# Sparse adjacency products by half blocks of 64 rows: two column parts of TensorE instead of one, in a two-layer graph network

## The chip, the cores and the metric

The kernel runs on one core of a Trainium2 chip. The core has five engines that work at once, each with its own in-order queue: TensorE (matmuls, in the profile PE, with its weight loads PEld), VectorE (DVE), ScalarE (ACT), GpSimd (POOL) and SyncE (SP), which only issues DMAs. The metric is the device time of one execution in microseconds, as the median over runs.

## What is computed

There are N = 2708 nodes with D = 256 features. Layer 0 is a dense graph product with an almost empty adjacency matrix (about 0.3 % of its entries and the diagonal are set):

```
support = adj @ x
x = layernorm(x + relu(concat([x, support]) @ weight + bias))
```

Layer 1 takes the result through two steps. In each, `Xf` goes through R, the adjacency with its identity, rows normalized, and `Xa` goes through an attention matrix A that keeps, in each row, only the largest probabilities whose mass reaches 0.9:

```
for n in range(2):
    A  = top_p_attention(Xa, W1, W2, W3)      # softmax, cut at mass 0.9, rows normalized
    Xf = R @ Xf
    Xa = A @ Xa
    Z  = Z + Xf @ U1[n].T + Xa @ U2[n].T
x = layernorm(x + layernorm(x + Z))
```

Here R = adj + I with each row divided by its sum. The kernel pulls the U1 products forward: with yf = x1 U1[1]ᵀ and v = x1 U1[0]ᵀ, the whole share of R is R (v + R yf). So there are two rounds over R with 256 columns each: s = 0 makes R yf and adds it to v, s = 1 makes R v.

## The kernel before

**Blocks.** Rows are cut into NB = 22 blocks of P = 128; the last one, EDGE, has 20 rows. All data is fp32. One fp32 matmul leaves two records in the trace.

**Stage 0 (layer 0).** For each block m the dense products of adj run on PE (`adj_product`), while DVE looks which 128 x 128 column groups are occupied (`name_columns`): for each block m of 128 rows, and for each of the 128 x 21 other nodes, whether any of the block's rows uses it. DVE then picks the occupied names out in rounds of eight (`Lists.take`, CAP = 160 names a part, two lists: blocks 0 to 15 and 16 to 21). POOL joins the parts to one list a block (`Lists.end`) and loads it back as `ix`: up to 7 columns (CC) of 128 (CW) node names. So R's block of 128 rows needs at most 896 columns instead of 2708.

**Step 1.** For each of the 22 attention blocks: logits on PE, the cut on DVE, transposes of the kept probabilities on PE (`turn`), their copy on ACT (line 530), products with x1 on PE (`products`, line 564). Beside them POOL gathers R's columns for each block by 7 indirect DMAs of 128 rows of 512 bytes from adj (`adj_gather`, line 367), and SP stores them packed (`adj_store`) in `adjc_d`. Each block ends in a chain `ends`: scale, transpose, projections to the queries and keys of step 2. `ya_pair` makes `ya` = Xa U2[1]ᵀ, two blocks at a time; 11 of them stand around the last block's chain.

**Step 2.** The loop `for per in range(NB + 2)` is a software pipeline. In period `per` the block `per - 2` is transposed and multiplied on PE, `per - 1` and `per` are searched and masked on DVE, and `per + 1` and `per + 2` are searched on ACT and exponentiated. A period has NG = 6 slots. The order of the work on each engine is written out by hand and is the program order.

**R in step 2.** A block of R is 8 matmuls of 128 x 128 by 128 x 256 (7 gathered column groups and the block's own diagonal one), 8 units in the text's count. `r_units(n)` places them in single units over the slots, as `units` says: two blocks ahead of the loop, one each in periods 0 and 1, 18 units a period in periods 2 to 9, none in period 10, 16 a period in periods 11 to 21. In slot 0 they stand ahead of the transposes. The rows of y that belong to the gathered columns are fetched by POOL: 7 indirect DMAs of 128 rows of 1024 bytes (`y_load`, line 719) into one of two slots of `yg`, for block m + 1 when block m begins. The adjacency part comes back by SP (`a_load`). When a block's last unit is placed, `r_out` is queued two slots on: it scales and adds the result, and in round 0 stores v. Round 1's first gather has to wait for all of v.

**Finals.** In round 1, `arrive` adds the parts; `final_slot` takes two rows' blocks a period through two layer norms. `middle` gives POOL two tensor operations a block (lines 1207 and 1208), in POOL's queue with the gathers; `stats` of both norms stand in slot 3 on DVE.

```
            n = n_r * (g + 1) // NG - n_r * g // NG
            ...
            if g == 0:
                if b_exp:
                    shift(b_exp, lg[0])
                r_units(n)
            ...
                turn(t_mul, g, ya, accs[t_mul], e2(t_mul))
```

**What sets the order.** DVE's two long operations of a period are `mask` (line 1088) and `below_level` (line 1023); `mask` releases the next block's transposes on PE, these the copies on ACT.

Of the kernel before, what the change touches and what calls it, by code (L numbers as in the profile page):

```python
# [38 lines left out]
CAP = 160  # L39
ML = 16  # L40
CW, CC = 128, 7
# [11 lines left out]
def gnn_two_layer_kernel(ctx: ExitStack, tc: tile.TileContext, N, xT_d, x_d, adj_d, w0_d, b0_d,  # L53
# [31 lines left out]
    assert NB == 3 * KS + 1 and CW == P and CAP % 8 == 0 and N < NB * P  # L85
# [16 lines left out]
    c.part_d = dram.tile([NB, KS, CAP + 1], FP, name="part_d")  # L102
    c.list_ds = [dram.tile([b - a, KS * CAP], I32, name="list_d") for a, b in ((0, ML), (ML, NB))]
    c.adjc_d = dram.tile([NB, CW, CC * P], FP, name="adjc_d")
# [15 lines left out]
    NF = 6 * NB + 4  # L120
# [28 lines left out]
def fast_path(ctx, tc, c, flags, fint, xT_d, x_d, w0_d, b0_d, w1_d, w2_d, w3_d, u1_d, u2_d, g_d, b_d):  # L149
# [43 lines left out]
    xT = big.tile([P, DC, N], FP, tag="Y", name="xT")  # L193
# [42 lines left out]
    def edge_sum(acc, n, stop=True, meanwhile=None):  # L236

        p = rows(EDGE)
        four = work.tile([P, 4, P], FP, tag="wT", name="four").rearrange("p k i -> p (k i)")
        nc.scalar.copy(four[:, :n], acc[:, :n])  # L240
        if meanwhile:
            meanwhile()
        whole = ps_misc() if meanwhile else ps_acc()
        nc.tensor.matmul(whole[:p, :n], lhsT=fold[:, :p], rhs=four[:, :n], start=True, stop=stop)
        return whole
# [21 lines left out]
    names = room[:, :NB * (NB - 1)].rearrange("p (m c) -> p m c", c=NB - 1)  # L267
    at = NB * (NB - 1)
    ramp = room[:, at:at + NB]
    some = room[:, at + NB:at + 2 * NB]  # L270
    LROOM = 3 * P + 2 * CAP + 1 + KS * (CAP + 1)
    first_room = room[:, at + 2 * NB:at + 2 * NB + LROOM]
# [6 lines left out]
    ix = small.tile([P, NB, CC], I32, tag="ix", name="ix", bufs=1)  # L279
    nc.gpsimd.iota(ix.rearrange("p m c -> p (m c)"), pattern=[[0, NB * CC]], base=LAST, channel_multiplier=0)  # L280
    for i, (a, b) in enumerate(((0, ML), (ML, NB))):
        nc.gpsimd.dma_start(out=c.list_ds[i][:, :CW * CC].rearrange("m (p c) -> p m c", c=CC), in_=ix[:, a:b, :])
    before_m = small.tile([NB, 1], FP, tag="before_m", name="before_m", bufs=1)
# [3 lines left out]
    def name_columns(m):  # L287
        for h in range(2):
            nc.vector.tensor_reduce(some[:, h * KH:(h + 1) * KH], adj_of[m][h], AX.X, ALU.max,
                                    apply_absolute_value=True)  # L290
        nc.vector.tensor_scalar(some, some, 0.0, None, op0=ALU.not_equal)
        for a, b, o in ((0, m, 0), (m + 1, NB, -1)):
            if a < b:
                nc.vector.scalar_tensor_tensor(names[:, m, a + o:b + o], ramp[:, a:b], -float(m * P * NB),
                                               some[:, a:b], op0=ALU.add, op1=ALU.mult)

    class Lists:


        def __init__(self, a, b, flag, room):  # L300
            self.a, self.b, self.n, self.flag = a, b, KS * (b - a), flag
# [22 lines left out]
        def end(self):  # L324
# [9 lines left out]
            nc.gpsimd.dma_start(out=c.part_d[a:b].rearrange("m s k -> (m s) k"), in_=self.out[:n])  # L334
            nc.gpsimd.dma_start(out=self.all, in_=c.part_d[a:b])
            run = small.tile([NB, KS], FP, tag="run", name="run", bufs=1)[:b - a]
            to = small.tile([NB, KS], I32, tag="to", name="to", bufs=2)[:b - a]
# [4 lines left out]
            list_d = c.list_ds[a > 0]  # L342
# [5 lines left out]
            nc.gpsimd.dma_start(out=ix[:CW, a:b, :], in_=list_d[:, :CW * CC].rearrange("m (p c) -> p m c", c=CC))  # L348

    adj_rows = adj_d.rearrange("m p k i -> (m p k) i")  # L350
    staged = {}

    to_turn = []

    def name_y():
        while to_turn:
            m = to_turn.pop()
            nc.gpsimd.tensor_scalar(ix[:CW, m, :], ix[:CW, m, :], m * P * NB, P * NB - 1, op0=ALU.subtract, op1=ALU.min)

    def adj_gather(m):  # L360
# [4 lines left out]
        name_y()  # L365
        for i in range(CC):
            nc.gpsimd.indirect_dma_start(out=a[:CW, i, :], out_offset=None, in_=adj_rows,  # L367
                                         in_offset=bass.IndirectOffsetOnAxis(ap=ix[:CW, m, i:i + 1], axis=0))
        nc.gpsimd.tensor_tensor(a[:p, CC, :], a[:p, CC, :], ident[:p], op=ALU.add)
        to_turn.append(m)  # L370
        staged[m] = a

    def adj_store(m, h):

        i = (CC + 1) // 2
        if h == 0:
            nc.sync.dma_start(out=c.adjc_d[m, :, :i * P], in_=staged[m][:CW, :i, :].rearrange("p c i -> p (c i)"))
            return
        a = staged.pop(m)
        nc.sync.dma_start(out=c.adjc_d[m, :, i * P:], in_=a[:CW, i:CC, :].rearrange("p c i -> p (c i)"))  # L380
        nc.sync.dma_start(out=c.own_d[m, :rows(m), :], in_=a[:rows(m), CC, :])
# [64 lines left out]
    lists = Lists(0, ML, flags[:, NF - 4:NF - 2], first_room)  # L446
    for m in range(NB):
# [18 lines left out]
        if m == ML:  # L466
# [16 lines left out]
        if m >= ML:  # L483
            i = m - ML
            lists.take(CAP // 8 * i // (NB - ML), CAP // 8 * (i + 1) // (NB - ML))
    assert not weights
    lists.end()
    y_room = big.tile([P, DC * N], FP, tag="Y", name="yg")
    YW = 2 * (CC + 1) * D
    yg = y_room[:, :YW].rearrange("p (s c d) -> p s c d", s=2, d=D)  # L490
    spares = [y_room[:, YW + D * i:YW + D * (i + 1)] for i in range(4)]
    lists = Lists(ML, NB, flags[:, NF - 2:], yg[:, 1].rearrange("p c d -> p (c d)"))
# [216 lines left out]
    r_now = []  # L709
    r_in, a_in, y_in = {}, {}, {}  # L710
    arrived, loads, held = {}, {}, {}
    later = [[], []]
    ready = []

    def y_load(s, m):
        y = yg[:, m % 2]
        rows_d = (c.yf_d, c.v_d)[s].rearrange("p k d -> (p k) d")
        for i in range(CC):
            nc.gpsimd.indirect_dma_start(out=y[:CW, i, :], out_offset=None, in_=rows_d,  # L719
                                         in_offset=bass.IndirectOffsetOnAxis(ap=ix[:CW, m, i:i + 1], axis=0))  # L720
        y_in[s, m] = y

    def a_load(m):
        a = adjp.tile([P, KH, P], FP, tag="adj", name="adj_t")
        nc.sync.dma_start(out=a[:CW, :CC, :].rearrange("p c i -> p (c i)"), in_=c.adjc_d[m])
# [3 lines left out]
    def r_load(s, m):  # L729
# [5 lines left out]
        nc.sync.dma_start(out=y[:rows(m), CC, :], in_=(c.yf_d, c.v_d)[s][:rows(m), m, :])  # L735
        r_in[s, m] = a_in.pop(m), y

    def r_units(n):
        for _ in range(n):
            s, m = r_queue[0]  # L740
            p = rows(m)
            if not r_now:
                r_now[:] = [ps_misc(), 0]
                if m + 1 < NB:
                    r_load(s, m + 1)
            acc, k = r_now
            a, y = r_in[s, m]
            kw = CW if k < CC else p
            nc.tensor.matmul(acc[:p, :D], lhsT=a[:kw, k, :p], rhs=y[:kw, k, :], start=k == 0, stop=k == CC)  # L749
            r_now[1] += 1  # L750
            if k == CC:
                r_now.clear()
                r_queue.pop(0)
                r_in.pop((s, m))
                base = za_load(m) if s else v_load(m)
                later[1].append(lambda s=s, m=m, acc=acc, base=base: r_out(s, m, acc, base))
# [6 lines left out]
    def za_load(m):  # L763
# [6 lines left out]
        base = work.tile([P, D], FP, tag="in", name="base", bufs=3)  # L770
# [3 lines left out]
    def r_out(s, m, acc, base):  # L774
        p = rows(m)
        if s == 0:
# [3 lines left out]
            if m == NB - 1:  # L780
                r_load(1, 0)
        else:
            arrive(m, base, acc, rinv[:p, m:m + 1])

    def arrive(m, base, part, scale):

        p = rows(m)
        if base is None:
            h = base = held.pop(m)
        else:  # L790
# [940 lines left out]
```

## Time and profile before

| | us |
|---|---|
| median of 3 runs (lowest, highest) | 1311.74 (1306.66, 1311.86) |
| profiled execution | 1361.88 |
| its span | 1360.1 |
| mean granted TensorE clock | 0.969 |

Busy time by stage, from the windows view of the profiled execution (us):

| stretch | what | PE | DVE | ACT | POOL |
|---|---|---|---|---|---|
| 0 to 288 | layer 0 | 273.7 | 157.5 | 32.0 | 5.5 |
| 288 to 345 | first logits, U1 | 53.1 | 37.3 | 28.3 | 17.5 |
| 345 to 748 | step 1 | 381.7 | 295.0 | 222.9 | 218.2 |
| 748 to 1050 | step 2, to period 10 | 265.1 | 230.0 | 223.3 | 189.9 |
| 1050 to 1321 | step 2, periods 11 to 21 | 254.3 | 253.5 | 219.9 | 202.8 |
| 1321 to 1360 | the end | 22.2 | 24.9 | 7.5 | 1.5 |

A busy PE is not a PE at its peak: the end of a matmul is modelled and the records overlap. POOL's busy time leaves out a gap of 0.30 us before each gather.

### The profile page before, as it was taken

How to read it: one execution, taken by the hardware profiler on the slowest of the kernel's cores; microseconds unless marked ns; L12 is line 12 of the kernel's file. 1: busy time of each engine (PE TensorE's matmuls, PEld its weight loads, DVE VectorE, ACT ScalarE, POOL GpSimd, SP SyncE). 2: the span in 40 equal slices, each digit the busy share in tenths (PEclk: the TensorE clock that was granted, in tenths of full speed). 3: DMA queues.
4: the chain of work that ended last, by engine and by line, in shares of the span. 5: the costliest groups of instructions: out<-in, count | busy, mean ns of one | idle time of the engine just before them, and what ended most of it. 6: DMA issues, size and time to landing. Idle time of an engine off the chain costs nothing.

```text
span 1360.1 us, 18883 instructions
## 1 busy us (share of the span) xinstructions
PE 1250.1 (92%) x5764; PEld 895.5 (66%) x5764; DVE 998.1 (73%) x3406; ACT 733.8 (54%) x1337; POOL 635.2 (47%) x594
## 2 busy tenths in 40 slices
PE   8999999988999999999997959999996999999985
PEld 6877877733567777666774727766664776666763
DVE  2544545866888888877840469878877899999995
ACT  1011011035455565555553577877786898998931
POOL 1000000014554533777563177777743668888850
PEclk9999999989899999999998969999998999999997
DMA  6554545513222110232222245645543444554541
GB/s 186 163 176 155 166 155 160 165 54 117 81 92 67 55 57 10 89 94 95 69 73 74 68 150 157 188 140 175 172 111 109 148 159 143 171 181 151 169 111 33
DMA packets 101993, 166.27 MB, mean 122 GB/s; under 512 B 17394, under 2 KB 74358, under 8 KB 101882
## 3 DMA queue, kind: packets, MB, share of 16 engines
q1 hardware_dynamic: 75596, 108.91, 24.7%
q0 software_dynamic: 20544, 51.17, 13.6%
q10 hardware_dynamic: 5742, 4.89, 1.3%
q8 instruction: 48, 0.79, 0.2%
q14 instruction: 63, 0.52, 0.1%
HBM read 130.87 MB, written 34.03 MB: 121 GB/s over the span
## 4 chain that ended last, share of the span: by engine, by line
PE 67%; ACT 19%; DVE 6%; issue 4%; another core or an unknown queue 2%; DMA 0%; ACTq 0%; DVEq 0%
PE acc L564 22%; PE acc L257 15%; PE lg L507 8%; PE tr L527 5%; PE misc L749 5%; ACT e L969 4%; ACT e L966 3%; ACT e L844 3%; ACT wT L530 3%; PE acc L651 2%; PE acc L462 2%; PE misc L426 2%; PE misc L392 2%; PE acc L672 2%
## 5 line engine op out<-in xcount | busy, mean ns | idle before, releaser
L530 ACT COPY wT<-tr 128x512 f32<-128x512 f32 (+2 forms) x258 | 131.7, 518 | 254.7 <-PE tr L527 153.3
L564 PE MATMUL acc<-ya,wT 128*128 128x256 f32 (+1 forms) x924 | 234.6, 394 | 18.8 <-ACT wT L530 12.1
L564 PE MATMUL acc<-x,wT 128*128 128x256 f32 (+1 forms) x924 | 234.6, 393 | 13.2 <-ACT wT L530 12.9
L719 POOL DMA_INDIRECT yg<-v_d,ix x154 | 190.1, 1234 | 79.4 <-issue 32.3
L564 PEld LDWEIGHTS acc<-x,wT 128*128 128x128 f32 (+1 forms) x924 | 167.2, 192 | 87.8 <-issue 40.6
L719 POOL DMA_INDIRECT yg<-yf_d,ix x154 | 192.6, 1250 | 62.3 <-issue 36.2
L564 PEld LDWEIGHTS acc<-ya,wT 128*128 128x128 f32 (+1 forms) x924 | 169.8, 193 | 75.6 <-issue 28.1
L257 PE MATMUL acc<-y,adj_t 128*128 128x257 f32 (+1 forms) x924 | 208.4, 381 | 0.0
L367 POOL DMA_INDIRECT adj_t<-in_adj,ix x154 | 170.3, 1106 | 51.4 <-issue 42.4
L749 PE MATMUL misc<-yg,adj_t 128*128 128x256 f32 (+1 forms) x704 | 183.5, 395 | 11.4 <-issue 6.6
L257 PEld LDWEIGHTS acc<-y,adj_t 128*128 128x128 f32 (+1 forms) x924 | 171.8, 189 | 32.7 <-issue 8.9
L507 PE MATMUL lg<-k,q 64*128 64x512 f32 (+3 forms) x528 | 151.9, 602 | 29.7 <-issue 11.2
L749 PEld LDWEIGHTS misc<-yg,adj_t 128*128 128x128 f32 (+1 forms) x704 | 125.7, 191 | 61.7 <-issue 31.2
L527 PE MATMUL tr<-ident,e 128*128 128x128 f32 (+2 forms) x946 | 147.0, 274 | 2.3 <-DVE e L1088 2.3
L527 PEld LDWEIGHTS tr<-ident,e 128*128 128x128 f32 (+2 forms) x946 | 113.6, 139 | 41.5 <-issue 17.6
L334 POOL DMA_DIRECT2D part_d<-e x1 | 0.6, 576 | 286.2 <-DVE e L333 286.2
L966 ACT ACTIVATE e<-e,st 128x2708 f32<-128x2708 f32 (+1 forms) x43 | 113.6, 2641 | 0.1
L570 DVE MAX8 cand<-e 128x8 f32<-128x170 f32 (+1 forms) x352 | 87.6, 318 | 32.7 <-ACT e L514 15.4
L969 ACT ACTIVATE e<-e,st 128x2708 f32<-128x2708 f32 (+1 forms) x42 | 110.9, 2641 | 0.1
L439 ACT COPY x1T<-tr 128x256 f32<-128x256 f32 (+1 forms) x22 | 8.0, 364 | 186.6 <-PE tr L438 186.6
L1030 DVE MAX8 cand<-w 128x8 f32<-128x136 f32 (+1 forms) x440 | 106.2, 285 | 0.0
L507 PEld LDWEIGHTS lg<-k,q 64*128 64x128 f32 (+1 forms) x528 | 39.3, 183 | 64.2 <-issue 35.6
(237 smaller groups left out, 1762.9 us busy)
## 6 DMA issues: line engine op xcount, KB each, us to landing
adj_t<-in_adj SPq DMA_DIRECT2D x44, 704.0 KB
adj_t<-adjc_d SPq DMA_DIRECT2D x44, 448.0 KB
adjc_d<-adj_t SPq DMA_DIRECT2D x22, 256.0 KB
base<-za_d SPq DMA_DIRECT2D x41, 128.0 KB
adjc_d<-adj_t SPq DMA_DIRECT2D x22, 192.0 KB
xt<-in_x ACTq DMA_DIRECT2D x21, 128.0 KB
x_d<-x SPq DMA_DIRECT2D x21, 128.0 KB
x1b_d<-xb SPq DMA_DIRECT2D x21, 128.0 KB
```

The costliest lines, as they stand in the source:

```text
L257: nc.tensor.matmul(acc[:p, :n], lhsT=halves[k // KH][:kw, k % KH, :p], rhs=y[:kw, k, :n], start=k == 0, stop=stop and k == NB - 1)
L367: nc.gpsimd.indirect_dma_start(out=a[:CW, i, :], out_offset=None, in_=adj_rows, in_offset=bass.IndirectOffsetOnAxis(ap=ix[:CW, m, i:i + 1] ...
L507: nc.tensor.matmul(lg[:p, h, :b - a], lhsT=q[o, t * P:t * P + p], rhs=keys[s][o, i, :b - a], start=True, stop=True)
L527: nc.tensor.transpose(tr[:kw, k % 4, :p], e[:p, k * P:k * P + kw], ident[:p, :p])
L530: nc.scalar.copy(wT[:, :full, :p], tr[:, :full, :p])
L564: nc.tensor.matmul(acc[:p, :D], lhsT=wT[:kw, k % 4, :p], rhs=y[:kw, k, :], start=k == 0, stop=k == NB - 1)
L570: nc.vector.max(dst[:p, i * 8:(i + 1) * 8], src[:p, i * step:i * step + w])
L719: nc.gpsimd.indirect_dma_start(out=y[:CW, i, :], out_offset=None, in_=rows_d, in_offset=bass.IndirectOffsetOnAxis(ap=ix[:CW, m, i:i + 1], ...
L749: nc.tensor.matmul(acc[:p, :D], lhsT=a[:kw, k, :p], rhs=y[:kw, k, :], start=k == 0, stop=k == CC)
L966: nc.scalar.activation(scr[:b.p, :N], e, AF.Relu, bias=b.nz, scale=b.l[k], accum_out=b.relu)
L969: nc.scalar.activation(scr[:b.p, :N], e, AF.Sign, bias=b.nz, scale=b.l[k], accum_out=b.sign)
L1030: nc.vector.max(b.cand[:p, 8 * i:8 * i + 8], low[:p, SEG2 * i:SEG2 * (i + 1)])
```

## The change

R's block of 128 rows is taken as two parts of 64. Each part has a column list of its own, of at most 4 x 128 names. On PE the two parts' matmuls stand in turn, one for PSUM rows 0 to 63 and one for rows 64 to 127, so on two column parts of the array; the own diagonal group stays one 128 x 128 matmul. A block has then 4 + 4 gathered column groups of 64 instead of 7 of 128. What goes with it:

- Three lists instead of two, of 9, 9 and 4 blocks with twice the rows; CAP falls from 160 to 96, so 12 rounds a list instead of 20. `Lists.end` is split into `end`, `gather`, `join` and `columns`, which stand apart in the program.
- `adj_gather` makes 8 gathers of 256-byte rows instead of 7 of 512-byte rows (4 for EDGE); the packed adjacency is 256 KB a block instead of 448 KB.
- `y_gather` makes 8 gathers of 128 x 1024 bytes a block (4 for EDGE) instead of 7, all in step 2 but those of round 0's first two blocks, as before.
- `r_block` places a whole block in one slot, after that slot's transposes, instead of units in every slot; `r_slots` says which slots. Block m loads m + 2 when it has been placed, into the slot of `yg` that it has read. Round 0 now ends in period 10, slot 4; round 1 has one block in period 11, three in 12, and two a period (slots 1 and 4) after that.
- The last block's chain of step 1 runs ahead of the `ya_pair`s; 5 of these follow after the first logits of the loop, 6 stand in period 0, one a slot. The buffers `e4` and `scr` in their tile come only with period 1 (`fifth`).
- The `stats` of the second norm move from slot 3 to slot 4.

```diff
-CAP = 160
-ML = 16
-CW, CC = 128, 7
+CAP = 96
+LISTS = ((0, 9), (9, 18), (18, 22))
+HP = 64
+CW, CC = 128, 4
+NQ = 2 * CC
...
+        def columns(self):
+            a, b = self.a, self.b
+            for g in range(2):
+                nc.gpsimd.tensor_scalar(ixa[:CW, a + g:b:2, :], ix[:CW, a + g:b:2, :], 2, g, op0=ALU.mult, op1=ALU.add)
+            for m in range(a // 2, b // 2):
+                own = ix[:CW, 2 * m:2 * m + 2, :]
+                nc.gpsimd.tensor_scalar(own, own, m * P * NB, P * NB - 1, op0=ALU.subtract, op1=ALU.min)
...
+    def parts(m):
+        return [(k, g, 2 * k + g) for k in range(CC) for g in range(2 if rows(m) > HP else 1)]
...
-        for i in range(CC):
-            nc.gpsimd.indirect_dma_start(out=a[:CW, i, :], out_offset=None, in_=adj_rows,
-                                         in_offset=bass.IndirectOffsetOnAxis(ap=ix[:CW, m, i:i + 1], axis=0))
+        flat = a.rearrange("p k i -> p (k i)")
+        for k, g, i in parts(m):
+            nc.gpsimd.indirect_dma_start(out=flat[:CW, HP * i:HP * (i + 1)], out_offset=None, in_=adj_rows,
+                                         in_offset=bass.IndirectOffsetOnAxis(ap=ixa[:CW, 2 * m + g, k:k + 1], axis=0))
...
+    def y_gather(s, m, y):
+        rows_d = (c.yf_d, c.v_d)[s].rearrange("p k d -> (p k) d")
+        for k, g, i in parts(m):
+            nc.gpsimd.indirect_dma_start(out=y[:CW, i, :], out_offset=None, in_=rows_d,
+                                         in_offset=bass.IndirectOffsetOnAxis(ap=ix[:CW, 2 * m + g, k:k + 1], axis=0))
...
-    def r_units(n):
-        for _ in range(n):
-            s, m = r_queue[0]
-            p = rows(m)
-            if not r_now:
-                r_now[:] = [ps_misc(), 0]
-                if m + 1 < NB:
-                    r_load(s, m + 1)
...
-            nc.tensor.matmul(acc[:p, :D], lhsT=a[:kw, k, :p], rhs=y[:kw, k, :], start=k == 0, stop=k == CC)
...
+    def r_block():
+        s, m = r_queue.pop(0)
+        p = rows(m)
+        acc = ps_misc()
+        a, y = r_in.pop((s, m))
+        flat = a.rearrange("p k i -> p (k i)")
+        for k, g, i in parts(m):
+            w = min(p, HP)
+            nc.tensor.matmul(acc[HP * g:HP * g + w, :D], lhsT=flat[:CW, HP * i:HP * i + w], rhs=y[:CW, i, :],
+                             start=k == 0, stop=False)
+        nc.tensor.matmul(acc[:p, :D], lhsT=a[:p, CC, :p], rhs=y[:p, NQ, :], start=False, stop=True)
+        if m + 2 < NB:
+            r_load(s, m + 2)
+        base = za_load(m) if s else v_load(m)
+        later[1].append(lambda: r_out(s, m, acc, base))
...
+    second.join(nc.gpsimd)
+    second.columns()
...
-            acc = edge_sum(acc, D, meanwhile=ya_pair)
+            acc = edge_sum(acc, D)
...
-        ya_pair()
         f()
-    ya_pair()
     for t in range(3):
         exps2(blocks[t], 2, *logits(1, t, 2))
-        ya_pair()
-    while y_pairs:
-        ya_pair()
...
         if i == 3:
-            for k, f in enumerate(new + finals):
+            for k, f in enumerate(new):
                 f.stats(k)
+        if i == 4:
+            for k, f in enumerate(finals):
+                f.stats(len(new) + k)
...
-    each = NB * (CC + 1)
-    first = 2 * (CC + 1)
-    units = {0: CC + 1, 1: CC + 1}
-    rest = each - first - sum(units.values())
-    units.update({p: rest * (p - 1) // 8 - rest * (p - 2) // 8 for p in range(2, 10)})
-    units.update({p: each * (p - 10) // 11 - each * (p - 11) // 11 for p in range(11, 22)})
+    first = 2
+    r_slots = {0: (), 1: (2, 5)}
+    r_slots.update({p: (1, 4) for p in range(2, 11)})
+    r_slots[11] = (5,)
+    r_slots.update({p: (1, 4) if p > 12 else (1, 3, 5) for p in range(12, 22)})
...
-    r_units(first)
+    while len(y_pairs) > NG:
+        ya_pair()
...
     for per in range(NB + 2):
+        if per == 1:
+            fifth()
...
-                r_units(n)
...
+            if g in r_slots.get(per, ()):
+                r_block()
...
+            if per == 0:
+                ya_pair()
...
+            if per == 0 and g >= NG - first:
+                r_block()
```

## The prediction

> **What bounds the kernel now.** I read the windows by stage first, then the costliest groups on the page, then the timelines of POOL, DVE and PE in one late period of step 2, since all that the change does to the products lies in step 2 (748 to 1360). In the groups, the products that are to become cheaper stand beside the gathers that feed them:
>
> ```profile
> L719 POOL DMA_INDIRECT yg<-v_d,ix x154 | 190.1, 1234 | 79.4 <-issue 32.3
> ...
> L719 POOL DMA_INDIRECT yg<-yf_d,ix x154 | 192.6, 1250 | 62.3 <-issue 36.2
> ...
> L749 PE MATMUL misc<-yg,adj_t 128*128 128x256 f32 (+1 forms) x704 | 183.5, 395 | 11.4 <-issue 6.6
> ```
>
> The reader should see two costs of like size: 183.5 us of PE for R, and 382.7 us of POOL for its y, with 141.7 us of idle before the gathers. Is that idle free time? The timeline of POOL with DVE's two long operations (start, length, engine, line) says mostly no:
>
> ```profile
> 1144.79 0.95 POOL L719 DMA_INDIRECT yg<-v_d,ix  x1 [0.30 <-issue]
> ...
> 1145.56 3.04 DVE L1088 SCALAR_TENSOR_TENSOR e<-w,st,e 128x2720 f32<-128x2720 f32 x1
> ...
> 1146.04 3.38 POOL L719 DMA_INDIRECT yg<-v_d,ix  x1 [0.30 <-PE acc L564]
> ...
> 1149.72 0.95 POOL L719 DMA_INDIRECT yg<-v_d,ix  x1 [0.31 <-issue]
> ...
> 1151.56 3.04 DVE L1023 SCALAR_TENSOR_TENSOR w<-e,st 128x2720 f32<-128x2720 f32 x1
> ...
> 1152.22 3.21 POOL L719 DMA_INDIRECT yg<-v_d,ix  x1 [0.30 <-issue]
> ```
>
> A gather costs 0.95 and a constant 0.30 before it, so 1.25 us; the one that meets a long DVE operation ends 0.8 us after that operation does and loses 2.43 or 2.26 us. In this period (1145 to 1170) POOL has 14 gathers (17.5), 4.7 of such loss and four tensor operations of the finals (about 3.0 over a normal gap): 25.2 us, and the period, from mask to mask, is 25.2 us. POOL is full. It is not what PE waits for yet, as blocks' last gathers end some 5 us before their first product. PE and ACT have another loop, seen in the same period: mask ends at 1148.6, then
>
> ```profile
> 1148.64 1.99 PE L564 MATMUL acc<-ya,wT 128*128 128x256 f32 x8
> ...
> 1150.47 1.03 PE L749 MATMUL misc<-yg,adj_t 128*128 128x256 f32 x4
> ...
> 1151.34 0.60 PE L527 MATMUL tr<-ident,e 128*128 128x128 f32 x4
> ...
> 1151.97 0.58 ACT L530 COPY wT<-tr 128x512 f32<-128x512 f32 x1 [2.64 <-PE misc L749]
> ```
>
> R's two units in slot 0 stand between mask and the transposes that ACT waits for. So the late periods have two limits at 25.2: this loop, and POOL.
>
> **What the Trainium skill says.** "SBUF — State Buffer", section "SBUF: two separate sides": GpSimd writes the descriptors of its own DMAs, and a VectorE operation that holds the shared port locks it out until it ends. The trace agrees (3.38 against 0.95 us). "Perfetto Trace Analysis", section "Per-instruction lifecycle", wants GpSimd timed from start to start; so I use 1.25 and not 0.95. "TensorEngine Tiling (Array Packing)", section "Key Properties": different tiles of the array run in parallel, and a change of tiling mode drains it. The trace has column parts of 32, for EDGE in layer 0, against the full width:
>
> ```profile
> 29.08 10.02 PE L257 MATMUL acc<-y,adj_t 128*128 128x257 f32 x44
> ...
> 276.62 4.66 PE L254 MATMUL acc<-y,adj_t 128*20 128x257 f32 x44 [3.53 <-issue]
> ```
>
> Both have 44 records; the second, half of it at half clock, takes less than half. Parts do run side by side. No run here shows parts of 64.
>
> **The change, part by part.**
>
> *Products on PE.* Back to back a record starts every 0.216 us, so a matmul is 0.43 and a block 8 x 0.43 = 3.46 us. After: four pairs at 0.43 and the own group 0.43, 2.16 us, and two changes of mode. After the 64-row logits the first record comes 0.09 late and the next 0.10 late, so 0.2 each: 2.56 us. Saved: 0.9 a block, 40 us of PE over 44 blocks. From both sides: with free changes 57 us; if the halves do not overlap, 9 x 0.43 + 0.4 = 4.3 us, a loss of 37. I take 40. None of it is time by itself: PE has gaps in step 2. What reaches the path is slot 0, now without R: 4 records, 0.87 us in a late period, 6 records, 1.3 us, in an early one. Against it a whole block delays `products` in slots 1 and 4 by 2.6 us, which ACT's long activations (2.64 us each) cover there; without that cover it costs 1.2 us a slot over the 3 units there now.
>
> *Gathers of y.* 8 instead of 7 a block, 4 for EDGE: 344 instead of 308, 36 x 1.25 = 45 us more on POOL. Periods: early, 16 x 1.25 + 5.2 = 25.2 us, against 18 units now, 15.75 x 1.25 + 5.2 = 24.9. Early periods last 26.2 on average (836.9 to 1046.9), so nearly nothing is won or lost. Late, 16 x 1.25 + 4.7 + 3.0 = 27.7 against 25.2: +2.5 a period. Two slots of yg let POOL run at most two blocks ahead, so PE waits in `r_block` soon after period 12, which takes three blocks. Behind PE's wait stand the transposes, behind these ACT's copies and DVE's next mask.
>
> *The sum of POOL from block 2's first gather (776.0) to the last (1309.4).* Now 294 gathers, 368 us; losses to DVE 382.7 - 308 x 0.946 = 91; finals 28 (13.9 + 13.8): 487 of 533, so 46 idle, 21 of them between the rounds. After: 328 gathers, 410; the same 91 and 28; and between the rounds what can't be avoided, the landing (1.5, estimated from the packets of the gathers before), the block 2.6, two slots to `r_out` 8, the store and load 2: 14. Sum 543. The first of these gathers waits for block 0, now in period 0, slot 4, which I put at 780. So the last gather ends at 1323; landing and block bring 1327. From R's last product to the end now 1360.1 - 1316.7 = 43.4; it moves from slot 5 to slot 4, +4. End 1374, +14 on the span, 1376 on the profiled execution's 1361.9.
>
> *The last block's chain ahead of the ya pairs.* It is late now by the pairs between its steps: the logits of line 507 at 759.7 could come at 752. DVE's first search at 763 moves to 755. The 19 us of pairs are partly hidden by ACT and DVE in period 0, at 6 x 0.58 = 3.5 us of ACT. Worth 5 to 8 us at period 1, but R's gathers then set the pace from 780, so I count 0 with POOL bound and 7 without.
>
> *Lists, adjacency, SP, stats.* Rounds of names: 36 instead of 40 at 1.1 us, 12 instead of 20 of them in step 1, where PE (17 us a block) is the longer: 0; without that cover, 9 us won. The wait of DVE at 292 for `part_d` (5.0) goes, before a DVE wait of 11.8 for ACT that takes it up: 0. Adjacency gathers 172 instead of 154, +22 us of POOL in step 1, where it is busy 218 of 403: 0. The `join` of the second list puts 7 scatters (some 2.2 us apart) ahead of the first gathers; stores stand 4 slots later, SP waits there and nobody for it. Bytes of `a_load` fall. Stats in slot 4 give the finals on POOL 4 us more: 0.
>
> *To the median.* The profiled execution is 50 us above it. If the two shrink alike the forecast is 1311.7 + 14 = 1326. If the 50 us come out of waits in step 2 in proportion (612 of 1360 us, so 22), POOL's idle falls to 24 and the change costs 36: 1348. I take in between, 1332.
>
> **Rivals.** *POOL has room (28 %), faster.* If gathers cost 1.1 us or less outside the profiled execution, 16 fit into 25.2 (17.6 + 7.7 = 25.3). That is the point from which it decides. Then: 7 at the start, 9 x 1.3 in early and 11 x 0.87 in late periods, 28 us: 1284. For it: the missing 50 us, and R's products never wait for a gather in late periods. Against: the spacing is constant to 0.01 us and the engine never pauses. *POOL absorbs it (12 %), same.* The 46 us idle take the 45 us; the last gather ends where it does now: 1312. Against: the gap between the rounds and the two-block limit. *Halves one after the other (5 %), slower:* PE +37 on top of POOL, 1350. For it only that the trace shows parts of 32, not 64.
>
> **Numbers.** POOL binds: 55 %, 1332, own range 1319 to 1352. Faster by over 0.5 %: 0.28; within 0.5 %, about what a measurement of this kernel can tell from no change: 0.12; slower 0.60. The range from 1284 to 1352 leaves out about 1 in 10 on each side.
>
> **What would show it.** POOL without idle from period 1 to the last gather, late periods near 27.7, PE waiting before R's first product of a block and ACT and DVE behind it; L749's group (r_block's line) near 110 us; two records of a pair starting together. Wrong, if late periods stay under 25.2 or gathers follow each other faster than 1.25.

## The result, and the profile after

The changed kernel takes 1371.85 us (median of 4 runs, 1369.1 to 1374.35), the kernel before 1311.8 (4 runs, 1306.66 to 1312.17): a ratio of 1.0471, 95% interval 1.0446 to 1.0497. It is 60 us slower; 1332 was forecast, with 1352 as the end of the range. Its profiled execution took 1369.5 us (span 1367.7), so this record lies 2 us under its median, where that of the kernel before lay 50 us above. Record against record the change costs 8 us; run against run 60. That difference is the first thing to explain.

The groups of the page after, for R's products and their gathers:

```profile
L752 POOL DMA_INDIRECT yg<-yf_d,ix x172 | 205.0, 1192 | 105.7 <-PE misc L784 63.5
L752 POOL DMA_INDIRECT yg<-v_d,ix x172 | 207.5, 1206 | 68.4 <-issue 33.6
...
L784 PE MATMUL misc<-yg,adj_t 128*64 128x256 f32 (+1 forms) x688 | 120.8, 425 | 34.0 <-DMA yg<-v_d,ix 25.3
```

POOL has 412.5 us of gathers instead of 382.7; the products of the parts take 120.8, and the own groups (line 786, 88 records) 34.2 more, against 183.5. PE now waits more for rows. Three of its waits (engine, line, what ended the wait: us in total, times, longest):

```profile
...
PE misc L784 <- DMA yg<-v_d,ix: 25.3, 22, 3.1
PE misc L415 <- DMA xT<-in_xT: 15.8, 1, 15.8
PE misc L784 <- DMA yg<-yf_d,ix: 8.3, 13, 2.3
```

The second of these three has nothing to do with R. Here is the timeline of a late period after (start, length, engine, line), to set beside the one shown of before:

```profile
1163.57 3.04 DVE L1129 SCALAR_TENSOR_TENSOR e<-w,st,e 128x2720 f32<-128x2720 f32 x1
...
1164.82 2.61 POOL L752 DMA_INDIRECT yg<-v_d,ix  x1 [0.30 <-DMA yg<-v_d,ix]
...
1169.96 3.04 DVE L1064 SCALAR_TENSOR_TENSOR w<-e,st 128x2720 f32<-128x2720 f32 x1
1170.23 3.60 POOL L752 DMA_INDIRECT yg<-v_d,ix  x1 [0.30 <-issue]
1171.84 1.52 PE L784 MATMUL misc<-yg,adj_t 128*64 128x256 f32 x12
...
1175.38 0.95 POOL L752 DMA_INDIRECT yg<-v_d,ix  x1 [0.31 <-issue]
1175.63 0.91 PE L784 MATMUL misc<-yg,adj_t 128*64 128x256 f32 x2 [2.27 <-DMA yg<-v_d,ix]
...
1190.85 3.04 DVE L1129 SCALAR_TENSOR_TENSOR e<-w,st,e 128x2720 f32<-128x2720 f32 x1
```

From the start of one mask to that of the next, an interval in what follows, it is 27.3 us. POOL goes from gather to gather, 1.25 us apart (1174.13, 1175.38, 1176.63 and on); the two that meet DVE's long operations take longer. PE places six products (twelve records) and stops 2.3 us for the next column. This interval and the two before it last 27.3 us each although the mean granted clock of TensorE was 0.87, 0.94 and 1.00 in them. So they do not hang on PE's pace; POOL, which has no pause, is the bound, as forecast.

### The profile page after: what moved, and what is told of

Read it like the earlier page. It is cut to its first block, busy times and chain, and to the rows that moved or that the text cites. A ratio compares the mean times of both kernels' runs of the same rounds, so it can differ in the third digit from the quotient of the medians.

```text
span 1367.7 us, 19110 instructions
## 1 busy us (share of the span) xinstructions
PE 1230.9 (90%) x5839; PEld 842.8 (62%) x5839; DVE 993.9 (73%) x3403; ACT 737.3 (54%) x1337; POOL 683.5 (50%) x663
## 3 DMA queue, kind: packets, MB, share of 16 engines
q1 hardware_dynamic: 76546, 95.32, 21.6%
## 4 chain that ended last, share of the span: by engine, by line
PE 74%; DMA 9%; ACT 6%; DVE 4%; issue 4%; POOL 3%; ACTq 0%; POOLq 0%; DVEq 0%
PE acc L599 26%; PE acc L259 15%; PE lg L542 9%; PE tr L562 6%; PE misc L784 5%; DMA yg<-v_d,ix 4%; DMA yg<-yf_d,ix 3%; PE acc L686 2%; POOL yg L752 2%; PE misc L786 2%; PE acc L486 2%; PE misc L449 2%; PE misc L415 2%; DMA xT<-in_xT 1%; PE misc L734 1%
## 5 line engine op out<-in xcount | busy, mean ns | idle before, releaser
L752 POOL DMA_INDIRECT yg<-yf_d,ix x172 | 205.0, 1192 | 105.7 <-PE misc L784 63.5
L752 POOL DMA_INDIRECT yg<-v_d,ix x172 | 207.5, 1206 | 68.4 <-issue 33.6
L599 PE MATMUL acc<-x,wT 128*128 128x256 f32 (+1 forms) x924 | 230.5, 388 | 0.0
L392 POOL DMA_INDIRECT adj_t<-in_adj,ixa x172 | 176.6, 1027 | 59.6 <-issue 46.9
L542 PE MATMUL lg<-k,q 64*128 64x512 f32 (+3 forms) x528 | 158.3, 625 | 42.5 <-ACT e L884 34.8
L784 PE MATMUL misc<-yg,adj_t 128*64 128x256 f32 (+1 forms) x688 | 120.8, 425 | 34.0 <-DMA yg<-v_d,ix 25.3
L784 PEld LDWEIGHTS misc<-yg,adj_t 128*64 128x64 f32 (+1 forms) x688 | 54.5, 148 | 103.0 <-DMA yg<-v_d,ix 41.0
```

Of the source, the lines that this page charges most:

```text
L392: nc.gpsimd.indirect_dma_start(out=flat[:CW, HP * i:HP * (i + 1)], out_offset=None, in_=adj_rows, in_offset=bass.IndirectOffsetOnAxis(ap=i ...
L542: nc.tensor.matmul(lg[:p, h, :b - a], lhsT=q[o, t * P:t * P + p], rhs=keys[s][o, i, :b - a], start=True, stop=True)
L599: nc.tensor.matmul(acc[:p, :D], lhsT=wT[:kw, k % 4, :p], rhs=y[:kw, k, :], start=k == 0, stop=k == NB - 1)
L784: nc.tensor.matmul(acc[HP * g:HP * g + w, :D], lhsT=flat[:CW, HP * i:HP * i + w], rhs=y[:CW, i, :], start=k == 0, stop=False)
```

## The experiments

The kernels of one group of runs ran on one chip; each group also timed the kernel before. In the first group it took 1366.9 us, in the three later ones 1311.75, 1311.9 and 1310.5. Times are compared within a group, or between groups in which the kernel before took the same to 1.5 us.

**The kernels themselves, again.** No edit.

> The kernel before, once more and unchanged, with its own records. Its timed executions took 1306.7 to 1312.2 us, but the one that was profiled first took 1361.9 us, 50 us more. Theory A (that execution was an odd one, and its step 2 held about 50 us that the timed ones do not have): this record has a span near 1310 us, and its late periods of step 2 are then shorter than 25.2 us. Theory B (recording makes the kernel before slower and leaves the changed one alone): the span is near 1360 us again while the timed median stays near 1311 us.

> The changed kernel once more and unchanged, timed beside the kernel before on one chip. On the chip of the first four runs the kernel before took 1366.9 us (1311.8 where the change was first timed), and ScalarE stood still for 8 to 22 us at the same places of its program (its 277th, 459th and 829th instruction) in both variants of the changed kernel, each time until a train of 16 to 32 gathers on POOL had ended. Theory F (such trains hold back what ScalarE needs to go on, and a chip differs in how much): if the kernel before is near 1367 here, the changed kernel is near 1525 (the 1510 of the kernel with the three-dimensional xT, and 16 for the start); if before is near 1312, it is near 1372 and has no such stall. Rival (the chip costs both kernels the same 55 us): 1427.

> The kernel before once more, for its records on the chip of these runs. Theory F: ScalarE's longest stall outside layer 0 is about 8 us, at its 743rd instruction, at the end of a train of 14 gathers, if the time is near 1367, and there is no stall over 5 us if the time is near 1312.

In the first group the kernel before took 1367.4 (ratio 0.9996, 0.9967 to 1.0025), in the second 1310.8; the changed kernel took 1373.6 there (ratio 1.0462, 1.0432 to 1.0493). Neither theory A nor B of the first run holds. The recorded execution of the first group, 1376.2, lies among the others (1361.4 to 1377.3), so recording adds nothing that can be seen; the chips differ. The record that the forecast was made from most likely comes from a chip like the first group's: its span is like theirs, and its intervals follow that group's record to 0.1 us in many places (26.12, 27.55, 26.05 against 26.11, 27.55, 26.15). What differs can be read from ScalarE's waits. The record before:

```profile
ACT wT L530 <- PE tr L527: 153.3, 94, 5.4
ACT wT L530 <- issue: 35.0, 17, 4.1
...
ACT wT L530 <- remote: 20.6, 6, 8.2
```

The same program on the second group's chip:

```profile
ACT wT L530 <- PE tr L527: 223.3, 132, 5.9
```

"issue" and "remote" are waits that end with nothing that the record holds, 55.6 us together. In the second record ScalarE has no such wait after 300 us. The sum is no account of the 50 us, since the waits for PE's transposes are 70 us longer in the second record. Where the 51 us between the spans lie can be read from the stages: 14 in step 1 (first to last masking, line 635: 384.9 and 370.5), 17 from there to the first mask of step 2, 18 in the ten intervals that follow the first (24.17 us each for seven of them; 26.2 on average in the first record), and none in the late ones.

So only the records of the second group (spans 1309.1 and 1371.5) show the change:

| stretch | before | after | difference |
|---|---|---|---|
| to step 1's first masking | 323.5 | 340.4 | +16.9 |
| step 1, to the last masking | 370.5 | 370.9 | +0.4 |
| to the first mask of step 2 | 81.1 | 85.6 | +4.5 |
| first interval between masks | 30.6 | 33.9 | +3.3 |
| the next ten | 241.2 | 243.7 | +2.5 |
| the twelfth | 24.2 | 37.9 | +13.7 |
| the other nine | 213.0 | 234.0 | +21.0 |
| from the last mask to the end | 25.0 | 25.1 | +0.1 |

By POOL: its first gather of step 2 that waits for a block of R starts at 753.5 before and 784.2 after; from there to the end of the last gather are 506.6 and 536.7; after that, 49.0 and 50.6. The expectation that tied the stalls of ScalarE to the chip held as far as it was put to the test: with the kernel before near 1312 the changed one takes 1373.6, and ScalarE has no wait after 300 us that ends with nothing. On a chip of 1367 the changed kernel itself was not run.

**The loads of xT.** The first row of the table is a part of the diff that was not in the forecast at all:

```diff
-    xT = big.tile([P, DC, N], FP, tag="Y", name="xT")
+    xT = big.tile([P, YT], FP, tag="Y", name="xT")[:, :DC * N].rearrange("p (c n) -> p c n", n=N)
```

SyncE's seven issues of these loads on the timeline, and its waits; before (second group), then the changed kernel:

```profile
0.75 3.70 SPq L196 DMA_DIRECT2D xT<-in_xT  x7
```

```profile
0.75 20.96 SPq L200 DMA_DIRECT2D xT<-in_xT  x7
...
SPq L200 <- DMA xT<-in_xT: 18.2, 6, 3.3
```

Six of the seven wait for the one before to land. Two kernels test the cause: the changed one with three dimensions again, and the kernel before with a flat tile.

```diff
-    xT = big.tile([P, YT], FP, tag="Y", name="xT")[:, :DC * N].rearrange("p (c n) -> p c n", n=N)
+    xT = big.tile([P, DC, YT // DC], FP, tag="Y", name="xT")[:, :, :N]
```

> The changed kernel, with the tile that xT is loaded into declared in three dimensions again (128 x 2 x 2816, of which the first 2708 columns of each half are used) instead of a flat row cut and refolded; the room stays as large. Theory S (the flat tile makes each of the seven loads of xT wait for the one before it: they were issued 3.3 to 3.6 us apart there, 0.4 us apart before): the loads are issued within 5 us again, the first products go on without the 15.9 us gap, and the time falls by 14 to 17 us, to about 1356. Rival (the loads merely move, and the adjacency loads behind them on SP's queue set the start anyway): 0 to 4 us, so 1368 to 1372.

> The changed kernel with the three-dimensional tile for xT, as in the second run, now to be read beside a kernel before of about 1312 us. The sum of the two records made on one chip (spans 1309.1 and 1371.5) is: POOL's first gather of step 2 after block 0's products starts at 753.5 before and 784.2 after (+30.7: 16 from the seven loads of xT, 15 from R's first two blocks standing behind the last block's chain), the stretch from there to its last gather's end is 506.6 and 536.7 (+30.1: 34 more gathers, less the idle they fill), and 49.0 and 50.6 follow. Theory S: the 16 us come back whole, 1357 (1354 to 1360). Rival (the stretch that POOL fills starts no earlier, since something else sets it): 1366 to 1374.

> The kernel before with nothing changed but the tile of xT, declared as one flat row per partition and refolded, as the change does. Theory S (each load of xT then waits for the one before it): 14 to 17 us slower than before, all of it ahead of 40 us. Rival (hidden by layer 0's other loads): 0 to 4 us.

In the third group the three-dimensional tile gives 1358.5 (ratio 1.0359, 1.0324 to 1.0395), 15 us less than the changed kernel's 1373.6 of the second group (the kernel before took the same in both), and the loads go out together:

```profile
0.75 3.75 SPq L200 DMA_DIRECT2D xT<-in_xT  x7
```

That is theory S. The flat tile alone does nothing, though: 1310.25 (0.9996, 0.9981 to 1.0011), issues in 3.71 us; this expectation failed. Of the three forms that ran, only the flat row that is cut out of a longer one and refolded makes the loads wait. That form was not put into the kernel before, and why it makes them wait is not shown.

In the first group the same kernel took 1510.0 us (1.1046, 1.0996 to 1.1096), 151 more than in the third. Its timeline at the longest stall:

```profile
403.61 0.19 ACT L648 ACTIVATION_READ_ACCUMULATOR e<-e,nmax 128x1 f32 x1
...
421.61 0.95 POOL L392 DMA_INDIRECT adj_t<-in_adj,ixa  x1 [0.30 <-issue]
425.39 0.58 ACT L565 COPY wT<-tr 128x512 f32<-128x512 f32 x1 [21.59 <-remote]
```

ScalarE stands 21.6 us with its input ready, while POOL ends a train of 24 gathers, and goes on 2.8 us after the last. What it lacked is not in the record.

**The number of gathers.** In the kernel before, an eighth gather a block into a column that nobody reads (`y_load`); in the changed one, the eighth left out and its column zero, so that those names are missing from R's products.

```diff
+        nc.gpsimd.indirect_dma_start(out=eighth[:CW], out_offset=None, in_=rows_d,
+                                     in_offset=bass.IndirectOffsetOnAxis(ap=ix[:CW, m, 0:1], axis=0))
```

```diff
         for k, g, i in parts(m):
+            if i >= 7:
+                continue
```

> The kernel before, with an eighth gather of y for every block (its first list again, into a column that nobody reads): 44 gathers more on POOL, no other engine has more work. Theory P (POOL's gathers set the pace of step 2, now and before): 40 of them lie in the stretch that POOL fills, so 40 x 1.25 = 50 us at most, 30 to 50 us, 1342 to 1362. Theory E (TensorE and ScalarE's loop sets the pace before, POOL has room): within 6 us of before, 1306 to 1318.

> The changed kernel without the eighth of its eight gathers of y for every block; the column of y that it filled holds zeros instead, so the names of that part are left out of R's products (which are all still issued). 43 or 44 gathers fewer on POOL. Theory P: 30 to 50 us less than the changed kernel, 1322 to 1342. Theory Q (what costs is that a block's products come in one slot and wait there, and POOL is not the bound): within 10 us of the changed kernel, 1362 to 1374.

The eighth gather costs the kernel before 45 us (1411.85 against 1366.85; 1.0342, 1.0311 to 1.0372), and its late intervals go from 25.2 to 27.7, by just two gathers of 1.25. That is theory P; TensorE and ScalarE's loop does not hide more gathers. Both kernels ran on the slower chip; on the other this was not measured. The other run (1470 to 1494) says nothing: it was in the first group too, without the changed kernel beside it, and shows the same stalls of ScalarE (22.9 us at 423).

**One slot.** The kernel before with a block's eight products placed together:

```diff
-            n = n_r * (g + 1) // NG - n_r * g // NG
+            n = (CC + 1) * (g in slots.get(per, ()))
```

> The kernel before with nothing but the placing of R's products changed: a block's seven gathered products and its own one follow each other in one slot of a period (two blocks a period, three in periods 2 and 6 of the first round), still 128 columns wide and still with seven gathers. Theory P (the number of gathers is what costs): within 10 us of before. Theory Q (products in one slot make TensorE wait for the whole block's rows, and hold the free of its room back): 15 to 40 us slower than before.

1341.1 (1.0219, 1.0195 to 1.0244): theory Q holds for this form, +29 us. The early intervals are shorter (23.04 for most, with 2 blocks instead of 2.25), the late ones 27.6 to 30: PE waits 24.7 us for rows of v, and POOL, which never stood over 0.3 us there before, pauses 2.5 to 2.8 us in most of them. A block now needs all its rows at once and gives its room back at once; that this is the cause is argued, not tested.

**R's first two blocks, and the slots.** The changed kernel with these blocks ahead of the ya pairs; then with both edits; then with the eighth gather left out as well; then, all gathers back, with other slots.

```diff
+    for _ in range(first):
+        r_block()
     while len(y_pairs) > NG:
         ya_pair()
...
-            if per == 0 and g >= NG - first:
-                r_block()
```

```diff
-    r_slots = {0: (), 1: (2, 5)}
-    r_slots.update({p: (1, 4) for p in range(2, 11)})
-    r_slots[11] = (5,)
-    r_slots.update({p: (1, 4) if p > 12 else (1, 3, 5) for p in range(12, 22)})
+    r_slots = {0: (3,), 10: (1,), 11: (2, 5)}
+    r_slots.update({p: (1, 4) for p in range(1, 10)})
+    r_slots.update({p: (1, 4) for p in range(12, 22)})
```

> The changed kernel with R's first two blocks back where the kernel before has them: ahead of the pairs of ya and of the first tries of step 2, not in the last two slots of period 0. Theory P (POOL fills the time from these products to its last gather, so an earlier start is a gain in full): the products start near 759 instead of 783, and the time falls by 15 to 24, to 1348 to 1358. Rival (the late start of POOL costs nothing, since the rounds are paced by the slots of the periods): 1368 to 1374.

> Both of these edits in the changed kernel. If both theories hold, they add up: 1332 to 1342, and what is left over the kernel before (20 to 30 us) is the price of the eighth gather of a block.

> Both edits, and y's eighth gather of a block left out (its column of y is zeros, so the names of that part are missing from R's products, which are all issued). Theory P (the eighth gather is the rest of the loss): 41 gathers fewer on a full POOL, the late periods fall from 27.3 to 24.8 to 25.2 us and the time to 1295 to 1315. Theory Q (what is left is the products in one slot, as in the kernel before with one slot a block, whose late periods were 27.6 to 29 us with seven gathers): late periods stay above 27, 1325 to 1342.

> The kernel with both edits (three-dimensional xT, R's first two blocks early; 1349 us) and its slots moved to follow: one block in slot 3 of period 0, two in periods 1 to 9, the last of the first round in period 10's slot 1, two of the second round in period 11 and in each period after it (three in none). Theory P (POOL fills the time, its idle of 16.7 us in period 1 and of 17 us between the rounds is what is lost): POOL waits less than 5 us in periods 0 and 1, period 12 falls from 38 to about 27 us, and the time falls by 8 to 18, to 1331 to 1341. Rival (the periods of step 2 are already as short as DVE and ScalarE let them be): 1345 to 1352.

| changed kernel with | us | ratio to before (95%) |
|---|---|---|
| first blocks early | 1366.1 | 1.0425 (1.0392 to 1.0458) |
| xT and first blocks | 1349.3 | 1.0299 (1.0266 to 1.0331) |
| the same, 7 gathers | 1321.5 | 1.0090 (1.0056 to 1.0123) |
| xT, first blocks, slots (fourth group) | 1338.6 | 1.0211 (1.0185 to 1.0237) |

The early blocks alone give 7.5 us, not 15 to 24: POOL starts at 759.4 instead of 784.2, gathers two blocks to 781.3, and then stands 16.7 us, since block 2 has its slot only in period 1. With the slots moved that idle is 6.5 us (777.4 to 783.9; under 5 was expected), the interval of 37.6 becomes 26.6, and the time falls by 10.7, inside the expected range. The edits to xT and to the first blocks add up (24.3 us together), and without the eighth gather 27.8 us go, between theory P (34 to 54) and Q (7 to 24). One early and one late interval of that kernel in the windows view (stretch, its length; busy us and instructions of PE, its loads, DVE, ACT and POOL; clock, DMA share, GB/s):

```profile
907.80:930.30 22.50, 20.89 (x116) 14.15 (x115) 20.99 (x77) 19.92 (x34) 17.81 (x15) 1.00 0.55 159
...
1128.40:1154.00 25.60, 22.79 (x114) 14.72 (x114) 23.70 (x86) 22.29 (x41) 21.32 (x19) 0.93 0.50 149
```

The early one is 1.7 us shorter than the 24.17 of before, and all ten sum to 233.4 instead of 241.2. Only part of this can be the gain of the cheaper products: the kernel before with one slot has 23.04 with the same two blocks in an interval, which leaves 0.5. Nor is it there wherever POOL has room: four of the ten are 22.5 us, but five are 24.0 to 24.2, and in each of these POOL pauses 1.1 us or more. What holds them is not shown.

The late one stops at 25.6, expected were 24.8 to 25.2. POOL is still without a pause in it (19 instructions, no idle but the 0.30 before a gather), and the gathers that meet DVE's long operations are these:

```profile
1128.89 3.39 POOL L755 DMA_INDIRECT yg<-v_d,ix  x1 [0.30 <-issue]
...
1135.09 3.59 POOL L755 DMA_INDIRECT yg<-v_d,ix  x1 [0.30 <-issue]
```

They lose 5.1 us over 0.95 each; in the interval of 27.3 shown above the two lost 4.3. With 14 gathers of 1.25 and 2.9 for the finals this makes 25.5, so POOL alone accounts for the 25.6: two gathers fewer won 1.7 and not 2.5, because more was lost beside DVE.

**Is POOL the bound before?** Two kernels made from before put R's first two blocks ahead of the chain and then spread the products over more periods.

```diff
     r_load(0, 0)
+    r_load(0, 1)
+    r_units(2 * (CC + 1))
+    for f in later[1]:
+        f()
+    later[1] = []
...
-    units = {0: CC + 1, 1: CC + 1}
+    units = {0: 2 * (CC + 1)}
...
-    units.update({p: rest * (p - 1) // 8 - rest * (p - 2) // 8 for p in range(2, 10)})
-    units.update({p: each * (p - 10) // 11 - each * (p - 11) // 11 for p in range(11, 22)})
+    units.update({p: rest * p // 8 - rest * (p - 1) // 8 for p in range(1, 9)})
+    units.update({p: each * (p - 9) // 12 - each * (p - 10) // 12 for p in range(10, 22)})
```

The second one has `rest * p // 9 - rest * (p - 1) // 9` in periods 1 to 9, and the second round as before.

> The kernel before with R's first two blocks ahead of the pairs of ya and of the last block's chain (about 725 us instead of 753), two blocks in period 0, the rest of the first round in periods 1 to 8 as dense as before, and the second round in 12 periods (10 to 21) instead of 11. Theory P (POOL's stretch sets the end before too): it starts 20 to 25 us earlier, the late periods have 12.8 gathers instead of 14 and fall from 25.2 to about 23.7, and the time falls by 6 to 15, to 1297 to 1306. Theory E (TensorE and ScalarE's loop sets the late periods at 25.2): within 4 us of before.

> The same early start, but the rest of the first round spread over periods 1 to 9 (16 products a period instead of 18) and the second round as before. Theory P: the early periods fall from 24.17 to about 23 us, as they did in the kernel before with one slot (23.04), and the late ones stay at 25.2: 6 to 12 us less than before, 1300 to 1306. Theory E: within 4 us of before.

The first is slower, 1328.8 (1.0145, 1.0121 to 1.0170), which neither theory had; the second, 1314.1 (1.0030, 1.0012 to 1.0049), is 3.6 us over before and so within theory E's 4. Neither expected gain came. An early and a late interval of the kernel before (second group):

```profile
805.70:829.90 24.20, 23.89 (x115) 18.04 (x115) 21.09 (x77) 19.95 (x34) 19.33 (x17) 1.00 0.67 203
1096.30:1121.50 25.20, 23.80 (x112) 17.01 (x111) 23.58 (x87) 22.30 (x40) 20.84 (x19) 1.00 0.55 167
```

Two late intervals of the first kernel:

```profile
1140.10:1165.30 25.20, 23.01 (x108) 16.13 (x106) 23.20 (x86) 22.30 (x40) 20.85 (x19) 1.00 0.55 170
1165.30:1190.50 25.20, 23.45 (x110) 16.51 (x108) 23.21 (x87) 22.30 (x40) 9.54 (x12) 1.00 0.40 121
```

In the second POOL has half the work, and the interval is the same 25.2 us. So late periods have another limit at 25.2, and fewer gathers win nothing there. What makes this kernel slower lies earlier: its first mask is 8 us later, the first interval 7 us longer and the next ten 3.5. In the other kernel the early intervals do fall, from 24.17 to 23.31, 6.7 us over all ten; the first interval is 4.7 us longer and the first mask 6 us later, which uses it up. The fall of 0.86 us is what two products take (2 x 0.43), and two fewer stand in these periods, while 1.75 gathers would be 2.2; PE is busy 23.89 of the 24.20 above. So it is PE that most likely sets the early intervals of before; this was not tested by itself. No kernel of this study beats the kernel before.

## Why the prediction was wrong

**The step that failed is "To the median".** It had two readings of the 50 us: both kernels shrink alike (+14), or 22 come out of the waits of step 2 (+36); it took the middle. On the chip of the times the stretch that POOL fills lasts 506.6 us in the kernel before, not 533, so 27 of the 50 came out of it. The sum's 487 us of work then leave 20 idle, not 46, of which 17 lie between the rounds (969.8 to 986.8). The second reading was near this, the first and so the middle were not: the +14 on the span was the difference of two kernels, on two chips. With the same 543 set against 506.6, the same +4 at the start, and the forecast's 51 us behind the last gather against 49.0, the sum gives +43: 1355, still outside the range.

**The second error is a term that was left out:** the loads of xT, 15 us, which bring the sum to 1370. That this is near 1372 is in part luck, since the start came 11 us later than that sum has it, and the stretch was 6 us shorter. The edits to lists, adjacency and SyncE's order, costed at 0, did cost 0 (step 1: 370.5 and 370.9), but the new declaration of a tile was read for its size alone.

Point by point:

- *Products on PE.* A block whose rows are there takes 2.58 us, forecast 2.56, and 3.62 in the kernel before with one slot, forecast 3.46 (this measure takes in the last matmul's end). The records of a pair start together (782.8, 782.8, 783.3, 783.3). This agrees with the Trainium skill, "TensorEngine Tiling (Array Packing)", section "Key Properties", which has different tiles of the array run in parallel, now for parts of 64. The group's busy time, 155 us with the own products instead of 110, is off because half of the blocks (median 3.4 us) come in pieces behind their rows.
- *Gathers.* Late intervals are 27.3 us, forecast 27.7; early ones 24.4 on average, forecast 25.2 (and 24.17 before on the timed chip, not the 26.2 of the record). POOL's stretch is 536.7, forecast 543. The eighth gather is worth 28 us in the changed kernel (42 gathers at 1.25 would be 52) and 45 in the kernel before, there on the slower chip: in the late intervals the gathers that are left lose more to VectorE's long operations, and in the early ones POOL pauses, so that something else holds them. The gathers that meet these operations take 2.61 and 3.60 us here, against 3.38 and 3.21 before.
- *The start of the stretch.* Forecast 780, measured 784.2, but the 776 that it was set against is 753.5 on the chip of the times. Of these 30.7 us 16 are the loads (768.2 with xT mended). The rest is not a price of the two blocks alone: with these moved ahead as well POOL starts at 741.7, 12 us before the kernel before, but then stands 16.7 us for the slot of block 2. Placing and slots together measure 20 us (9.2 and 10.7, with xT mended); the forecast had 4, plus the three blocks of period 12 at nothing.
- *The chain ahead of the ya pairs.* Counted 0 with POOL bound; from the last masking of step 1 to the first mask of step 2 it takes 4.5 us more, not less.
- *The rivals.* POOL has room: no, the gathers keep 1.25 us in the timed chip's record too. POOL absorbs it: no, of its 46 us of idle 26 are not there on the chip of the times. Halves one after the other: no, the pairs start together.

One after the other the edits give back 15 us for xT and 9 for the place of the first blocks; on top of these two, 11 for the slots or 28 for the eighth gather. These sum to 63, and the two kernels lie 62 apart, but no kernel has all four edits, so that they add up is not shown. With the first two and without the eighth gather 10 us are left over the kernel before (1321.5 against 1311.9). The 25.2 us limit of the kernel before is not settled: in it no engine is busy over 23.8 us, and the loop of mask, products, transposes and copies that the forecast named was not tested by itself.

## What to carry to other kernels

Where a record lies above the timed runs, it may be of another chip: take one that agrees with them before making a sum of idle time from it, for the excess need not lie evenly over the stages. A stage with two limits at the same value gives nothing for relieving one, and takes the full price of loading it. Read the declared shape of a tile in a diff as you read its size: the same seven loads took 4 us or 21.

## What the runs showed of the hardware

- The same kernel took 1311 us on one chip and 1367 on another, and one version of the changed kernel 1358.5 and 1510.0. On the slower chip ScalarE stood still at the same three places of its program in two versions of the changed kernel (11 to 23 us each); in four of these six stalls it went on 2.8 to 3.4 us after a train of 14 to 24 gathers ended, in the other two inside a train. On the other chip trains of 56 and 156 gathers leave no such stall, and the kernel before with an eighth gather, with trains of 16 to 41 in step 2 on the slower chip, has none over 8 us; so the length of a train alone does not explain them. In the one of 21.6 us (404 to 425 us) the DMA queues carry only the packets of the gathers and of SyncE's transfers. The cause stays open.
- Column parts of 64 rows run in pairs at 2.58 us for 8 + 1 products, where eight of full width take 3.62.
- In three late intervals of the changed kernel, all of 27.3 us, the mean granted clock was 1.00, 0.94 and 0.87: it fell to half for 3.4 us (1148.6 to 1152.0) and for 6.8 us (1175.9 to 1182.7). In the late intervals of the kernel before it was 1.00. What sets it is not shown: the kernel with 7 gathers has such a time of half clock (1136.2 to 1139.5) in an interval in which PE waited for no rows.
